# Closing a mixture-of-experts layer in groups of four tiles by batch entry, with eight gather buffers and normed values on ScalarE

## The chip, the cores and the metric

The kernel runs on one core of one Trainium2 chip, all in 32-bit floats. The metric is device time in microseconds (us) of one execution, the median of repeated runs. A core has a matrix engine (TensorE, PE in the profile; its weight loads are PEld), a vector engine (VectorE, DVE), a scalar engine (ScalarE, ACT), a fourth engine that here mostly issues indirect DMAs (GpSimd, POOL), and a queue that issues the other DMAs (SyncE, SP). Each engine works through its own queue of instructions in order. Where an instruction needs what another engine or a DMA makes, it waits on a semaphore, and all that is queued behind it waits too.

## The reference, cut to what matters

The input x is 4 batch entries of 1024 tokens of 128 values. Four layers follow each other, and each has two steps, `x = layernorm(x + f(x))`:

```python
x = ln(x + L0_attn(x)); x = ln(x + L0_ffn(x))   # cumulative-sum attention; linear in 6-bit steps
x = ln(x + L1_attn(x)); x = ln(x + L1_ffn(x))   # state-space scan; 16 experts, 4 per token, and a shared one
x = ln(x + L2_attn(x)); x = ln(x + L2_ffn(x))   # causal attention, 16 heads; 8 experts, 2 per token
x = ln(x + L3_attn(x)); x = ln(x + L3_ffn(x))   # Toeplitz gated unit; 32 experts, 4 per token, and a shared one
```

`ln` subtracts a token's mean and divides by the root of its variance plus 1e-5. The step of concern is the end of `L1_ffn`: for every token the outputs of its four experts, weighted, are added to x (which holds the shared expert's output already), and the sum is normed:

```python
x[t] += sum(wk[t, i] * y[pos[t, i]] for i in range(4)); x[t] = ln(x[t])
```

## The kernel before, in words

**Tiling.** The 4096 tokens are 32 tiles of 128 tokens (partitions) by 128 values. They are held by quarters of the sequence: quarter q has tokens 256q to 256q+255 of all four batch entries, which is eight tiles (QT), the first two of batch entry 0, the next two of entry 1, and so on. Part a is quarters 0 and 1 (16 tiles, the first half of the sequence), part r is quarters 2 and 3. Causal attention of layer 2 takes one half at a time, batch entry by batch entry: `l2_attn(0)` needs part a, `l2_attn(1)` needs both.

**Experts by lists.** A router (`l1_route`, L775) gives every token four places in a list that is sorted by expert. Tokens are scattered into the list in HBM by indirect DMA (`spread`, `indirect`, L1325), the experts run over it in tiles of 128 rows, and their results lie in HBM (`l1ya` for part a, `l1yr` for part r; `yg` is the tile that they are written from). `collect` (L1441) fetches them back. For each tile of tokens it takes one buffer "yt" of a pool `yp`, issues four gathers on POOL (indirect DMA, recorded at L1327) and later four multiply-adds on DVE (L1452). The pool's size is how many tiles can be under way: a gather into a buffer waits until the adds of the tile that had it before are done. `collect` issues the adds when a modelled landing time has passed, or when as many tiles are waiting as there are buffers, and a call of it adds all that it still has before it ends. `spaced(gen, 1, 2, 1.45)` (L1363) makes every gather wait for the landing of the one two before it; part r's gathers run so, part a's don't.

**Closing.** `l1_close` (L851) does this quarter by quarter: eight tiles collected, `norm` of the eight, one DMA that saves them in HBM (`xsave`, L858), and two times `turned` (L220), which is four PE transposes (L169) into a PSUM tile and one copy on ACT (L171) into xT, the transposed values that the next projections take.

**Norm.** `norm` (L189) takes a list of tiles. Per tile it has bn_stats and bn_aggr on DVE (L196, L197). `by="act"` takes the root on ACT (Sqrt, L200) and the reciprocal on DVE (L201); `by="dve"` takes Newton steps on DVE instead (L180 to L187, L204). Then the values: with `on_act=False`, one DVE instruction per tile (L213); with `on_act=True`, one small DVE instruction for all (`off`, L208) and one ACT instruction per tile (Identity with scale and bias, L211).

**What sets the order.** The program is recorded by generators that yield modelled costs. `mix(main, side, pace, drain)` (L242) records main and puts in as much of side as main's costs make due; `queued` (L232) keeps what is recorded from side behind what main has recorded so far on the same engine. A tile scheduler then orders each engine's instructions from these dependencies and a cost model. The stages around the change are written in `all` (L1957): at L1984 the shared expert and the experts of part a are the main work (`l1_experts`), beside which the chain of quarters 2 and 3 runs (`l2_norms`, `l0_ffn` L530, then `l1_attn` L648, both with `beside=True`). At L1985 `l1_close(a)` runs beside what is left of that chain and the making of layer 2's weights. Then comes `l2_attn(0)`, whose first PE work is transposes and projections of part a. At L1992 `l2_experts` (L1540) of layer 2's part a2 is the main work and `l1_close(r)` the side work; `l2_attn(1)` follows at L1999.

**Names in the steps.** In `l1_attn`, L669 forms the scan's inputs from a projection, L673 is the scan, L700 the residual add (two per quarter). In `l2_experts` a unit is one tile of the list: `gu` (PE, two products), `sg` (ACT, Silu, L1567), `hg` (DVE, L1569), four transposes into `tp`, `hT` (their copy, on ACT L171 or DVE L173 in turn), `yp` (PE); every four units `yg` is written (L1589) and a new list tile xg is transposed. `gu` and `sg` have two buffers, `hg` four, `hT` three. L979 adds an output bias to x inside `l2_attn`, L954 is its rotation, L933 to L935 are memsets of its value tile `va`, `sc` its scores. L1418 and L1419 read a count and branch over a rarely needed rest of the experts.

Of the kernel before, what the change touches and what calls it, by code (L numbers as in the profile page):

```python
# [30 lines left out]
QT = NT // NQT  # L31
# [9 lines left out]
E1, F1, NG1, TKG1, K1 = 16, 128, 4, 2, 4  # L41
# [33 lines left out]
class Kernel:  # L75
# [454 lines left out]
    def l0_ffn(self, qs, beside=False):  # L530

        nc, tc, x = self.nc, self.tc, self.x
        with ExitStack() as ctx:
            tp = self.pool(ctx, "l0ft", 4, right=True)
            qp = self.pool(ctx, "l0fq", 2, right=True)
            ps = self.side if beside else self.pool(ctx, "l0fps", 2, space=PSUM)
            tag = lambda t: "s" if beside else t
            for q in qs:
                t0 = q * QT
                xd = self.tile(qp, [P, QT, D], "xd")  # L540
                self.quantize(
                    tp,
                    xd.rearrange("p t d -> p (t d)"),
                    x[:, t0 : t0 + QT, :].rearrange("p t d -> p (t d)"),
                    QC // 32, beside,
                )
                yield (10.0,)

                lb = self.row["l0_b"].unsqueeze(1)
                if beside:  # L550
                    nc.gpsimd.tensor_tensor(
                        x[:, t0 : t0 + QT, :], x[:, t0 : t0 + QT, :], lb.to_broadcast([P, QT, D]), ALU.add
                    )
                for g in range(2):
                    xdT = self.tile(qp, [P, BLK], "xdT")
                    self.transposes(ps, xdT, [xd[:, g * 4 + k, :] for k in range(4)], tag=tag("tp"))
                    po = self.tile(ps, [P, 4, D], tag("po"))
                    if not beside:
                        self.mm(po, self.ident, lb.to_broadcast([P, 4, D]), True, False)
                    for k in range(4):  # L560
                        self.mm(po[:, k, :], xdT[:, k * P : (k + 1) * P], self.l0_wT, beside, beside or k == 3)
                    s = slice(t0 + g * 4, t0 + g * 4 + 4)
                    nc.vector.tensor_tensor(x[:, s, :], po, x[:, s, :], ALU.add)
                    yield (4.0,)
                self.norm(self.quarter(q), by="dve" if beside else "act", on_act=not beside)
                yield (6.0,)
                for g in range(2):
                    self.turned(ps, t0 + g * 4, tag=tag("tp"))
                yield (4.0,)
# [78 lines left out]
    def l1_attn(self, qs, beside=False):  # L648
        nc, tc, x, xT = self.nc, self.tc, self.x, self.xT
        tt, stt = nc.vector.tensor_tensor, nc.vector.scalar_tensor_tensor  # L650
        pw, wi, lh = self.l1_p, self.l1_w, self.l1_h
        rows = lambda a: a.rearrange("p (b t) -> p b t", b=B)
        steps = lambda a: a.unsqueeze(1).to_broadcast([P, B, TQ])
        with ExitStack() as ctx:
            tp = self.pool(ctx, "l1t", 2, right=True)
            ps = self.side if beside else self.pool(ctx, "l1ps", 2, space=PSUM)
            tag = lambda t: "s" if beside else "pu" if t == "pu" else "po"
            for q in qs:
                pu = []
                for h in range(2):  # L660
                    z = self.tile(ps, [P, BLK], tag("pu"))
                    self.mm(z, self.l1_b, xT[:, q * QC + h * BLK : q * QC + (h + 1) * BLK])
                    pu.append(z.rearrange("p (b t) -> p b t", b=B // 2))
                g = []
                for r in range(2):
                    b = self.tile(tp, [P, QC], "b")
                    for h in range(2):
                        hb = slice(h * B // 2, (h + 1) * B // 2)
                        tt(rows(b)[:, hb], pu[h], steps(wi[:, r, :])[:, hb], ALU.mult)  # L669
                    if q:  # L670
                        tt(rows(b)[:, :, 0], rows(b)[:, :, 0], lh[:, r, :], ALU.add)
                    s = self.tile(tp, [P, QC], f"g{r}")
                    nc.vector.tensor_tensor_scan(  # L673
                        s, self.l1_keep.rearrange("p b t -> p (b t)"), b, 0.0, ALU.mult, ALU.add
                    )
                    g.append(s)
                    yield (5.0,)
                if q + 1 < NQT:

                    ge = [rows(s)[:, :, TQ - 1] for s in g]  # L680
                    pr, pi = pw[:, 0, TQ - 1 :], pw[:, 1, TQ - 1 :]
                    u = self.tile(self.small, [P, 2, B], "lhu")
                    nc.vector.tensor_scalar(u[:, 0, :], ge[1], pi, self.l1_rho, ALU.mult, ALU.mult)
                    nc.vector.tensor_scalar(u[:, 1, :], ge[1], pr, self.l1_rho, ALU.mult, ALU.mult)
                    v = self.tile(self.small, [P, 2, B], "lhv")
                    nc.vector.tensor_scalar(v[:, 0, :], ge[0], pr, self.l1_rho, ALU.mult, ALU.mult)
                    nc.vector.tensor_scalar(v[:, 1, :], ge[0], pi, self.l1_rho, ALU.mult, ALU.mult)
                    tt(lh[:, 0, :], v[:, 0, :], u[:, 0, :], ALU.subtract)
                    tt(lh[:, 1, :], v[:, 1, :], u[:, 1, :], ALU.add)

                (tt if beside else nc.gpsimd.tensor_tensor)(rows(g[0]), rows(g[0]), steps(pw[:, 0, :]), ALU.mult)
                tt(rows(g[1]), rows(g[1]), steps(pw[:, 1, :]), ALU.mult)
                for h in range(2):
                    po = self.tile(ps, [P, 4, D], tag("po"))
                    for k in range(4):
                        c = slice((h * 4 + k) * P, (h * 4 + k + 1) * P)
                        for r in range(2):
                            self.mm(po[:, k, :], g[r][:, c], self.l1_c[:, r, :], r == 0, r == 1)
                    sl = slice(q * QT + h * 4, q * QT + h * 4 + 4)
                    tt(x[:, sl, :], po, x[:, sl, :], ALU.add)  # L700
                    yield (3.0,)
                self.norm(self.quarter(q), by="dve" if beside else "act", on_act=not beside)
                yield (6.0,)
                for h in range(2):
                    self.turned(ps, q * QT + h * 4, tag=tag("tp"))
                yield (4.0,)
# [144 lines left out]
    def l1_close(self, part, yp):  # L851

        nc, x = self.nc, self.x
        for q in range(part.q0, part.q0 + part.nq):
            yield from self.collect("l1", part, K1, yp, (q - part.q0) * QT, QT)
            self.norm(self.quarter(q))
            tl = slice(q * QT, (q + 1) * QT)
            nc.sync.dma_start(out=self.xsave[:, tl, :], in_=x[:, tl, :])  # L858
            yield (6.0,)
            for g in range(2):  # L860
                self.turned(self.side, q * QT + g * 4, tag="s")
                yield (1.5,)


# [1092 lines left out]
    def all(self):  # L1957
# [4 lines left out]
        with ExitStack() as ctx:  # L1962
            lgp = self.pool(ctx, "l2lg")
            self.l2_lg = self.tile(lgp, [P, NT, E2], "lg")
            with ExitStack() as early:

                self.l0_setup(early)
                self.l2_wr = self.load(lgp, self.ins["l2_wr"])
                with ExitStack() as room:
                    self.l0_room(room)  # L1970
                    self.run(self.l0_attn((0, 1)))
                    self.l1_setup()
                    self.zero_lists("l1")
                    self.run(self.l0_ffn((0, 1)))
                    self.run(self.l1_attn((0, 1)))

                    self.run(self.l1_route(a))
                    self.run(self.mix(self.l0_attn((2, 3)), self.spread("l1", a, K1)))
                self.zero_lists("l2", "l3")
                with ExitStack() as c2:  # L1980
                    wall = self.l1_wall(c2)
                    yp = self.pool(c2, "l1ya", 5, right=True)
                    side = self.chain(self.l2_norms(), self.l0_ffn((2, 3), True), self.l1_attn((2, 3), True))
                    self.run(self.mix(self.chain(self.l1_shared(a, self.l1_sw), self.l1_experts(a, wall)), side, 2.0, False))  # L1984
                    self.run(self.mix(self.abreast(self.l2_weights(), side), self.l1_close(a, yp)))  # L1985
# [237 lines left out]
```

## Time and profile before

| | |
|---|---|
| time, median of three runs | 1929.3 us (1927.78 to 1932.83) |
| the profiled execution's own time | 1937.33 us |
| its span in the profile | 1935.5 us |
| mean granted clock of TensorE | 0.896 |
| busy in the span | PE 1541.5, DVE 1199.2, ACT 900.6, POOL 690.3 us |
| gathers of part a (64) | start 459.3 to 557.3, median 947 ns each |
| adds of part a (64) | start 492.7 to 560.0, median 343 ns each |
| gathers of part r (64) | start 855.7 to 973.1, median 946 ns each |
| adds of part r (64) | start 892.5 to 980.4, median 346 ns each |
| first scores of `l2_attn(0)`, of `l2_attn(1)` | 574.44, 998.79 |

The times in the profile count from the start of the span of one execution. A row of a timeline has the start, the duration, the engine, the line of the kernel, the operation, what it writes and reads (names without buffer numbers), how many instructions run on end in the row, and in square brackets the idle time of that engine before it and what ended it. An engine that is idle before an instruction need not cost anything: it does so only where the work that sets the end passes through it. PE has the most busy time; where it is full, work of other engines beside it is hidden, and where it is not, the question is what it waits for.

### The profile page before, as it was taken

The page shows a single profiled execution, that of the slowest core. Times are in us where ns is not written, and L with a number is a line of the kernel's source. Part 1 is how long each engine was busy: PE and PEld are TensorE (multiplying, and loading weights), DVE is VectorE, ACT ScalarE, POOL GpSimd, SP SyncE. Part 2 cuts the span into 40 slices and gives each one's busy share as a digit, 9 for nine tenths or more (in the row PEclk, how much of TensorE's full clock was granted, in tenths as well). Part 3 has the DMA queues.
Part 4 walks back from the last instruction along what each step waited for, and adds up shares of the span by engine and source line. Part 5 has one row for each costly group of instructions (what it writes and reads, how often), then busy time and mean ns, then how long its engine had stood idle before and what let it go on. Part 6 is the DMA issues. An engine that isn't in the chain of part 4 may idle for free. (4 is left out here: it accounts for less than half of the span.)

```text
span 1935.5 us, 27095 instructions
## 1 busy us (share of the span) xinstructions
PE 1541.5 (80%) x9025; PEld 920.8 (48%) x9025; DVE 1199.2 (62%) x3491; ACT 900.6 (47%) x1349; POOL 690.3 (36%) x670
## 2 busy tenths in 40 slices
PE   7885677597847887989977878798798998999850
PEld 3332433385423345856632232333355757768650
DVE  8998698465766664635564565546442446866383
ACT  5876265243324554423336756564532236644330
POOL 2000148604630660265443000030536430567775
PEclk9897688798978998999988988898988999989985
DMA  9990002244430113632241000000452213425452
GB/s 297 288 288 10 1 17 86 87 126 133 159 129 18 60 63 129 183 96 73 78 137 32 1 1 1 2 23 1 159 213 83 66 28 93 141 68 167 122 147 61
DMA packets 215530, 187.10 MB, mean 97 GB/s; under 512 B 16528, under 2 KB 194064, under 8 KB 214864
## 3 DMA queue, kind: packets, MB, share of 16 engines
q1 hardware_dynamic: 194672, 142.29, 23.6%
q0 software_dynamic: 20704, 42.86, 7.3%
q8 instruction: 84, 1.38, 0.3%
q14 instruction: 70, 0.57, 0.1%
HBM read 88.49 MB, written 96.60 MB: 96 GB/s over the span
## 5 line engine op out<-in xcount | busy, mean ns | idle before, releaser
L1081 ACT ACTIVATE pr<-sc 128x1024 f32<-128x1024 f32 x288 | 279.4, 1021 | 175.2 <-PE sc L161 174.8
L161 PE MATMUL sc<-qm,kT 32*128 32x512 f32 (+3 forms) x1536 | 197.7, 559 | 16.7 <-ACT pr L1081 16.7
L161 PE MATMUL s<-pr,va 128*32 128x512 f32 (+3 forms) x1536 | 167.5, 532 | 19.0 <-DVE x L1019 10.2
L161 PE MATMUL gu<-ld,xgT 128*128 x640 | 165.1, 400 | 10.2 <-DVE hg L1812 5.9
L1087 DVE TENSOR_TENSOR pr<-pr,ld 128x512 f32<-128x512 f32 (+1 forms) x160 | 91.7, 581 | 105.6 <-ACT pr L1081 105.4
L161 PE MATMUL gu<-wall,xgT 128*128 x304 | 148.2, 612 | 2.0 <-ACT xgT L171 2.0
L161 PEld LDWEIGHTS sc<-qm,kT 32*128 32x128 f32 x1536 | 83.7, 194 | 112.4 <-issue 61.1
L161 PEld LDWEIGHTS gu<-ld,xgT 128*128 128x128 f32 x640 | 119.5, 198 | 34.7 <-DVE hg L1812 6.1
L1812 DVE TENSOR_TENSOR hg<-sg,gu 128x256 f32<-128x256 f32 x160 | 66.0, 417 | 92.0 <-ACT sg L1811 91.6
L173 DVE COPY hT<-tp 128x512 f32<-128x512 f32 x118 | 80.9, 686 | 66.2 <-PE tp L169 66.2
L1567 ACT ACTIVATE sg<-gu 128x512 f32<-128x512 f32 x76 | 45.4, 597 | 144.7 <-PE gu L161 143.6
L1811 ACT ACTIVATE sg<-gu 128x256 f32<-128x256 f32 x160 | 61.3, 385 | 107.7 <-PE gu L161 79.8
L171 ACT COPY xgT<-tp 128x512 f32<-128x512 f32 x99 | 58.0, 586 | 99.9 <-PE tp L169 99.8
L1327 POOL DMA_INDIRECT l1ra<-x,posl1a x64 | 79.8, 1246 | 61.3 <-DVE peq L1321 42.0
L1327 POOL DMA_INDIRECT l1rr<-x,posl1r x64 | 65.4, 1022 | 100.9 <-DVE posl1r L1302 70.8
L169 PEld LDWEIGHTS tp<-ld,hg 128*128 128x128 f32 x624 | 77.4, 141 | 49.0 <-issue 32.5
L1569 DVE TENSOR_TENSOR hg<-sg,gu 128x512 f32<-128x512 f32 x76 | 51.8, 682 | 78.9 <-ACT sg L1567 78.8
L1327 POOL DMA_INDIRECT l2rm<-x,posl2m x16 | 15.7, 983 | 236.8 <-DVE peq L1320 230.1
L169 PE MATMUL tp<-ld,hg 128*128 128x128 f32 x624 | 96.4, 275 | 3.7 <-DVE hg L1812 2.0
L1327 POOL DMA_INDIRECT l3ra<-x,posl3a x64 | 63.7, 996 | 93.3 <-DVE usedl3a L1315 51.0
L161 PEld LDWEIGHTS s<-pr,va 128*32 128x32 f32 x1536 | 37.1, 113 | 122.6 <-issue 78.4
L161 PE MATMUL yp<-ld,hT 128*128 x640 | 86.1, 276 | 2.3 <-DVE mv L197 1.5
(447 smaller groups left out, 3439.1 us busy)
## 6 DMA issues: line engine op xcount, KB each, us to landing
wall<-wall SPq DMA_DIRECT2D x16, 768.0 KB, 7.8
l3ra<-zero SPq DMA_DIRECT2D x1, 6144.0 KB, 25.5
ld<-in_l_w SPq DMA_DIRECT2D x2, 3072.0 KB, 10.6
wall<-we SPq DMA_DIRECT2D x24, 256.0 KB, 2.1
ld<-in_l_w SPq DMA_DIRECT2D x1, 6144.0 KB, 20.6
l1ra<-zero SPq DMA_DIRECT2D x1, 5120.0 KB, 19.6
l1rr<-zero SPq DMA_DIRECT2D x1, 5120.0 KB, 23.1
xg<-l3ra SPq DMA_DIRECT2D x20, 256.0 KB, 2.9
```

What stands on the lines that cost most here:

```text
L161: return self.nc.tensor.matmul(out, lhsT, rhs, start=start, stop=stop)
L169: nc.tensor.transpose(pt[:, k * P : (k + 1) * P], s, self.ident)
L171: nc.scalar.copy(dst, pt[:, : n * P])
L173: nc.vector.tensor_copy(dst, pt[:, : n * P])
L1081: nc.scalar.activation(pr, sc[h], AF.Exp)
L1087: nc.vector.tensor_tensor(d, d, cst["tril"].unsqueeze(1).unsqueeze(1).to_broadcast([P, 2, n, P]), ALU.mult)
L1327: ins = self.nc.gpsimd.indirect_dma_start(**kw)
L1567: nc.scalar.activation(sg, gu[:, 0, :], AF.Silu)
L1569: nc.vector.tensor_tensor(h, sg, gu[:, 1, :], ALU.mult)
L1811: nc.scalar.activation(sg, pg[:, :, 0, :], AF.Silu)
L1812: nc.vector.tensor_tensor(h[:, 2 * c : 2 * c + 2, :], sg, pg[:, :, 1, :], ALU.mult)
```

## The change

Three edits. The norms of quarters 2 and 3 in `l0_ffn` and `l1_attn` give their normed values on ScalarE (they keep the Newton steps on DVE). `l1_close` takes groups of four tiles: first the first four tiles (batch entries 0 and 1) of both quarters, then the last four (entries 2 and 3) of both; each group is collected, normed (values on ScalarE), saved and transposed on its own. The pool of gather buffers of part a has eight buffers instead of five; part r's keeps five.

```diff
@@ l0_ffn, and the same in l1_attn
-                self.norm(self.quarter(q), by="dve" if beside else "act", on_act=not beside)
+                self.norm(self.quarter(q), by="dve" if beside else "act", on_act=True)
@@ l1_close
-        for q in range(part.q0, part.q0 + part.nq):
-            yield from self.collect("l1", part, K1, yp, (q - part.q0) * QT, QT)
-            self.norm(self.quarter(q))
-            tl = slice(q * QT, (q + 1) * QT)
-            nc.sync.dma_start(out=self.xsave[:, tl, :], in_=x[:, tl, :])
-            yield (6.0,)
-            for g in range(2):
-                self.turned(self.side, q * QT + g * 4, tag="s")
+        for g in range(2):
+            for q in range(part.q0, part.q0 + part.nq):
+                t0 = q * QT + g * 4
+                yield from self.collect("l1", part, K1, yp, t0 - part.t0, 4)
+                self.norm([x[:, t0 + k, :] for k in range(4)], on_act=True)
+                nc.sync.dma_start(out=self.xsave[:, t0 : t0 + 4, :], in_=x[:, t0 : t0 + 4, :])
+                yield (3.0,)
+                self.turned(self.side, t0, tag="s")
                 yield (1.5,)
@@ all
-                    yp = self.pool(c2, "l1ya", 5, right=True)
+                    yp = self.pool(c2, "l1ya", 8, right=True)
```

In the order of the instructions after the change, POOL's gathers take the same places as before except that those of the last two tiles of part r stand behind the branch of L1419. On DVE the adds stand in other places, which the prediction names; t0 to t15 are a part's tiles in the order in which they are collected. SP has eight saves instead of four, and in `l2_experts` with the closing of part r ACT loads a table for Sqrt, or back from it, six times instead of two.

## Prediction

> **What bounds the kernel now.** I read the page's busy shares first, then busy time per 20-us window, then the timelines of PE, POOL and DVE in the two places where layer 1 is closed; the chain that ended last stays inside the last stage and says nothing here.
>
> ```profile
> PE 1541.5 (80%) x9025; PEld 920.8 (48%) x9025; DVE 1199.2 (62%) x3491; ACT 900.6 (47%) x1349; POOL 690.3 (36%) x670
> ```
>
> PE is the busiest engine, but a mean over stages doesn't price a closing. In the windows (window length, PE, PEld, DVE, ACT, POOL busy, then granted clock) the two closings differ:
>
> ```profile
> 520.00:540.00 20.00, 17.35 (x76) 11.03 (x76) 15.50 (x80) 5.75 (x11) 15.43 (x16) 0.91 0.78 281
> 540.00:560.00 20.00, 0.66 (x4) 0.42 (x4) 11.79 (x48) 1.50 (x3) 12.84 (x13) 0.57 0.36 107
> 560.00:580.00 20.00, 14.62 (x53) 6.64 (x54) 13.29 (x34) 5.86 (x8) 0.00 (x0) 0.75 0.17 68
> ...
> 930.00:950.00 20.00, 20.00 (x113) 13.92 (x111) 9.09 (x16) 6.94 (x13) 9.60 (x10) 1.00 0.31 82
> 950.00:970.00 20.00, 20.00 (x107) 13.46 (x106) 11.74 (x26) 5.60 (x10) 8.52 (x9) 1.00 0.15 41
> 970.00:990.00 20.00, 11.96 (x72) 9.09 (x71) 15.77 (x62) 6.26 (x9) 4.82 (x5) 0.83 0.40 118
> ```
>
> In the first half's closing (part a) PE stands still for 21 us while POOL gathers; in the second half's (part r) PE is full until about 980, so gathers, adds and norms lie beside l2_experts and only the tail after 980 is on the path. PE's timeline shows the hole (start, duration; in brackets the idle time and its releaser):
>
> ```profile
> 540.48 0.66 PE L169 MATMUL s<-ld,x 128*128 128x128 f32 x4 [0.68 <-ACT xT L171]
> 562.45 2.17 PE L169 MATMUL s<-ld,x 128*128 128x128 f32 x8 [21.31 <-DVE x L213]
> 564.41 4.94 PE L161 MATMUL s<-xT,w 128*128 128x512 f32 x8
> ```
>
> The named releaser is only the last link; behind it lie the last gather and its adds. POOL's stops in part a:
>
> ```profile
> 494.85 0.94 POOL L1327 DMA_INDIRECT yt<-l1ya,posl1a  x1 [9.52 <-DVE bn L196]
> ...
> 505.93 0.95 POOL L1327 DMA_INDIRECT yt<-l1ya,posl1a  x1 [1.30 <-DVE x L1452]
> ...
> 542.56 1.07 POOL L1327 DMA_INDIRECT yt<-l1ya,posl1a  x1 [2.05 <-DVE x L1452]
> ```
>
> From 459.3, 64 gathers at 1.25 us (their spacing where nothing stops them) would end at 539.4; the last starts at 557.30. So 9.5+1.3+2.1 us are waits for a buffer, about 5 us longer gathers, and the last add is at 560.05.
>
> **The change, part by part.**
>
> *Eight buffers in part a.* They remove the 9.5 and 1.3 us: t0 to t7 run 459.3 to 499.4, t8 to t11 until about 519.5. t12 then needs t4's buffer, hence t4's four adds. In the changed order of DVE these stand behind the residual adds (L700) of l1_attn's last quarter; before, 17 adds stood after that quarter's norms, at 540.34. So POOL's stop moves and may grow: what is late next is that quarter's chain.
>
> *Norms of the second half on ScalarE.* Eight L213 on DVE (2.14 us, at 501.65) become one L208 and eight L211. The trace has eight L211 in 3.19 us (at 100.38). Four such places: q2's and q3's in l0_ffn are hidden (after q3's at 463.06 PE waits for a weight load until 466.07). The one at 501.65 is not: DVE is free at about 503.4 and ACT does q2's L211 at 503.6 to 506.8, but then the first close group's table load (1.28), Sqrt (0.30) and four L211 (1.6) stand in ACT's queue ahead of the copies of q2's transposes, and that group's transposes in PE's queue. I get q3's first L669, behind them in PE's queue, at 518.2 instead of 508.65: +9.5. Given back: about 16 adds (4.3 us at 0.27, as 17 in 4.57 at 540.34) no longer lie inside that stretch, and up to 1 us of DVE's 4.19 of idle ahead of its first L700. The two L700 then come at about 530 and 533.6 (before 526.35 and 528.98). t4 is free at 535.9, t12's gathers run 536.1 to 541.1. t5 is free after the memsets and Newton steps (4.4 us, as at 533.85 to 538.29) and eight adds, at 542.7; t13 to t15 are 12 gathers, 15 us, last landing and add at 559.6 to 559.9. Before: 560.05. So POOL loses 13 us of stops and gains about the same at t12 and t13: −0.3.
>
> *Groups of four, batch order.* L1979's remaining adds are done earlier, −0.5 at the hole's end (four bn and adds in the tail instead of eight, against four L211 of 1.6 us for eight L213 of 2.2). Behind it stands one projection for one; the last group's transposes are ahead of the first scores in PE's queue, so that early batch entries lie ready changes nothing. +0.8 (0 to 2) for the longer norms inside l1_experts, where PE is at 14 to 18 of 20. Four saves more are 0.32 us each of SP's queue (the save at 987.55); behind one that waits for its norm stand, in part r, loads of l2_experts' rows, issued at 934.70 for the transposes of 946.70, so some 10 us early: 0, unless a norm is later than that. Part a: about **0, −4 to +4**.
>
> *Part r, five buffers.* The same order with the old pool. In the order in which tiles are now collected, gather t9 needs t4's adds, t10 t5's, t11 t6's, t12 t7's, t13 t12's, t14 t13's, t15 t8's. t4's adds stand behind the hg that ran at 927.89, so POOL stops until about 930.5 (its stops before: 9.15 us at 894.26, 8.38 at 955.17). From there 12 gathers lead to t12's first, four to its last; it lands 2.86 us later (855.68 to 858.54, where the gather two behind waits for it), its adds let t13 go, four gathers more, landing, add. With a spacing s that is 930.5 + 15s + 2.86 + 0.65 + 3s + 2.86 + 0.35 = 937.2 + 18s. s is 1.50 in the trace (the first 20 run 855.68 to 884.16; the later ones give the same without their stops), so t13 is added at 964.2. But the eight adds of t12 and t13 stand in DVE's queue *ahead* of t8's to t11's, between the hg of 943.57 and the hT of 955.65, so what is queued behind a waiting add is hg and hT of a PE that is full:
>
> ```profile
> 946.20 0.69 DVE L1569 TENSOR_TENSOR hg<-sg,gu 128x512 f32<-128x512 f32 x1 [1.96 <-ACT sg L1567]
> ...
> 952.79 0.69 DVE L1569 TENSOR_TENSOR hg<-sg,gu 128x512 f32<-128x512 f32 x1 [1.96 <-ACT sg L1567]
> ...
> 955.65 0.69 DVE L173 COPY hT<-tp 128x512 f32<-128x512 f32 x1 [0.74 <-PE tp L169]
> ```
>
> The rhythm is 3.05 us per unit. hg may be 3.35 us late (made 958.89 to 959.58, its gu buffer reused at 962.93) and hT 2.2 (955.65, wanted 958.50, 0.69 long). The hT of 949.55 goes behind t12's last add (956.2): 6.6 late, PE 4.4. That of 955.65 goes behind t13's (964.2): 8.5 late, PE **+6.4**, and a full PE doesn't make it up. At s = 1.28, the trace's shortest regular spacing, it is +2.4; at 1.65, the mean from 894.26 to 945.84 with its stops, +9.0.
>
> *Sqrt in part r.* Two norms of eight become four of four, and in l2_experts and its tail ScalarE loads a table six times instead of twice. The rows:
>
> ```profile
> 923.42 1.28 ACT L200 ACT_TABLE_LOAD   x1
> 925.06 0.30 ACT L200 ACTIVATE rstd<-mv,eps 128x8 f32<-128x8 f32 x1 [0.36 <-DVE mv L197]
> 925.90 1.28 ACT L1567 ACT_TABLE_LOAD   x1 [0.53 <-PE gu L161]
> ```
>
> Here the Trainium skill speaks against the change: the page "ScalarE: Activation LUTs" (What ACT_TABLE_LOAD costs) puts a switch at 1283 ns plus a drain of about 1380, 2.66 us in all, and its rules for kernel authors say to do all of one set before switching. By the page four more switches are 10.6 us of ACT, and each Silu behind one would come 2.7 late; by the row they are 5.1 us, with no drain to be seen beyond the 0.36 and 0.53 of idle, and the next Silu (927.19) is some 0.4 late while PE stays at 20.00 of 20. I take the row: ACT has 13 of 20 us free, 0 for two groups and +1 for the third, whose load, four L211 and transposes fall into the last units. By the page it would be +3.
>
> *Tail of r.* Four adds, norm and transposes instead of eight; ACT's L211 instead of L213; I have PE's first projection 9.1 us after the last yp, before 9.7 (979.90 to 989.59, 1.48 of it a weight load): −0.5. The last eight gathers move behind a branch on POOL; landed by about 981, before the experts end, some 6 us after 979.90: 0.
>
> **Sum.** Part a 0 (−0.3 −0.5 +0.8), part r +6.4 +1.0 −0.5: **+6.9**. On the profiled execution's own 1937.33 us (span 1935.5 and 1.83 around it) that is 1944.2. That execution lies 8.0 over the median of the three runs (1929.3); on the median the forecast is **1936.2**.
>
> **Rivals.** *Forecast as summed* (1932 to 1941): chance 0.50.
> *Not slower: the hole in part a closes earlier* (1929; 0.20). One mechanism: l1_attn's last quarter isn't held back by ACT, so t4's buffer is free when t11's gathers are through. Then POOL never stops there, the last gather ends up to 7 us sooner and PE's 21.3 becomes 14; −7 against part r's +6.9 is 0. The point is the start of part a's 49th gather: at 531 or before it wins all, at 536 nothing. For it: 13 us of stops are really there. Against it: table load and L211 ahead of q2's copies.
> *Slower still* (1943; 0.20). Part r's gathers at 1.65 (+9.5 for r) and part a's stop grows by 4: +13.5. For: that spacing is the trace's own beside a full PE; against: 4 us of it were waits for adds.
> *It does nothing* (1929 to 1932; 0.10): gathers at 1.28 when nothing else moves, +2.4 +0.5, and less if hg's slack is larger; the stop in part a only moved. [...]
>
> **How the numbers follow.** A measurement of this kernel tells 0.3% (5.8 us) from no change: 1923.5 to 1935.1. Faster needs the second and the fourth case together, 0.10; within are most of these two and a third of the first, 0.35; slower are the third and most of the first, 0.55. The range takes in half of the second case's spread below 1929 (1925) and reaches past the middle of the third (1944).
>
> **What would show it.** PE's idle before the transposes ahead of l2_attn(0): 21 right, 14 the rival. Part a's 49th gather at 536, after an L1452. q3's L669 at 518. In part r DVE waits for yt's landings between its hg, and PE loses some 6 us in 945 to 970; if it stays at 20.00 of 20, my part r is wrong. Six table loads in l2_experts, PE unmoved by the first four. The prediction fails above all if q2's chain slips by less than 9.5, or if part r's gathers run closer than 1.5.

## The result and the profile after

| | before | changed |
|---|---|---|
| median of 4 runs, us | 1931.07 (1927.78 to 1933.14) | 1950.78 (1950.57 to 1954.82) |
| profiled execution, own time / span | 1937.33 / 1935.5 | 1954.82 / 1952.8 |
| granted clock over the span | 0.896 | 0.891 |

The ratio is 1.0108 [1.0088, 1.0128]: the change costs about 20 us on this chip. The direction was forecast; the size was not (+5 to +7), and the time lies above the range. Later runs were on other chips, 16 to 18% slower, on which this cost is not seen in the whole time; the last section tells of it. Times of a kernel are therefore only set against `before` on the same chip, and lengths of stages are read within a trace. Every ratio with an interval is of the executions within 1.5% of the kernel's fastest, which on the slower chips, where they scatter by up to 3%, are 5 of 12 of the changed kernel and 21 of 23 of `before`, so that medians of all are given there too.

The page's busy line and the three windows around part r's closing, of the changed kernel (window; length; PE, PEld, DVE, ACT, POOL busy; granted clock, DMA share, GB/s):

```profile
PE 1544.0 (79%) x9025; PEld 924.8 (47%) x9025; DVE 1184.5 (61%) x3443; ACT 931.3 (48%) x1421; POOL 690.0 (35%) x670
```

```profile
930.00:950.00 20.00, 19.54 (x106) 13.03 (x104) 9.67 (x28) 11.06 (x19) 12.04 (x13) 1.00 0.28 80
950.00:970.00 20.00, 16.21 (x77) 11.22 (x78) 9.25 (x19) 3.93 (x7) 10.45 (x11) 0.83 0.25 63
970.00:990.00 20.00, 17.22 (x100) 12.22 (x99) 15.03 (x50) 10.03 (x16) 3.84 (x4) 0.98 0.19 56
```

The busy line hardly moved. In the windows, PE had 20.00 of 20 up to 970 before; now it loses some 4 us between 945 and 970, and what it does there runs at a lower clock. Milestones place the rest (us, from the timelines):

| | before | after | moved by |
|---|---|---|---|
| first scores of l2_attn(0), behind part a | 574.44 | 576.05 | +1.6 |
| first gate-and-up matmul of l2_experts | 863.89 | 863.65 | −0.2 |
| l2_experts to its last yp | 116.0 | 123.8 | +7.8 |
| last yp to the first scores of l2_attn(1) | 18.9 | 26.5 | +7.6 |
| first gather of l3yc, last stage | 1877.6 | 1892.6 | +15.0 |
| first to last gather of l3yc | 42.7 | 45.0 | +2.3 |

So part a's lateness is gone by 863; part r costs 15.4 us in two places of about equal size; and 2.3 come in a stage that the change doesn't touch.

**Inside l2_experts.** PE's timeline there (start, length, instruction; in brackets idle time and releaser):

```profile
948.94 0.60 PE L169 MATMUL tp<-ld,hg 128*128 128x128 f32 x4
953.79 2.08 PE L161 MATMUL yp<-wall,hT 128*128 x8 [4.25 <-DVE yg L1589]
955.66 3.35 PE L161 MATMUL gu<-wall,xgT 128*128 x4
...
959.29 1.06 PE L161 MATMUL yp<-wall,hT 128*128 x8
```

and DVE's:

```profile
951.56 0.35 DVE L1452 SCALAR_TENSOR_TENSOR x<-yt,wkl1r,x 128x128 f32<-128x128 f32 x1 [6.23 <-DMA yt<-l1yr,posl1r]
951.83 0.68 DVE L1569 TENSOR_TENSOR hg<-sg,gu 128x512 f32<-128x512 f32 x1
952.79 0.35 DVE L1452 SCALAR_TENSOR_TENSOR x<-yt,wkl1r,x 128x128 f32<-128x128 f32 x1 [0.28 <-DMA yt<-l1yr,posl1r]
953.05 0.68 DVE L1589 COPY yg<-yp 128x512 f32<-128x512 f32 x1
...
963.78 0.35 DVE L1452 SCALAR_TENSOR_TENSOR x<-yt,wkl1r,x 128x128 f32<-128x128 f32 x1 [1.64 <-DMA yt<-l1yr,posl1r]
```

DVE stands 6.2 us on the first add of t12, which its queue has ahead of the adds of t8 to t11; the gather for it began at 948.95 and landed only then. Behind t12's second add in the queue is the copy that empties yp (L1589), which has one PSUM buffer; PE cannot start the next yp until it has run. After 4.25 us without work PE is also slow: eight yp matmuls take 2.08 us instead of 1.06, four gate-and-up matmuls 3.35 instead of 1.88, together 2.5 us more, at a granted clock of 0.64 in 955 to 960. The third group's four transposes, which lay in the tail before, are in this stage now (1.05 us at 983.68 with 0.33 ahead). 4.25 + 2.5 + about 1 is the 7.8.

**In the tail.** PE again:

```profile
985.37 2.10 PE L161 MATMUL yp<-wall,hT 128*128 x16
995.85 0.86 PE L169 MATMUL s<-ld,x 128*128 128x128 f32 x2 [8.38 <-ACT x L211]
996.50 1.92 PE L161 MATMUL s<-xT,w 128*128 128x512 f32 x2
...
1006.66 4.39 PE L161 MATMUL s<-xT,w 128*128 128x512 f32 x6 [7.82 <-DVE rot L954]
```

The first projection is 9.03 us after the last yp (before 9.69), as forecast, although the transposes wait 8.4 us instead of 5.9: t14's and t15's adds start at 990.35, behind the branch of L1419 and va's memsets, with rows that landed long before. But two projections later PE stands still for 7.8 us, for want of a PSUM buffer that a rotation on DVE has to empty. DVE and SP's queue say why:

```profile
1005.21 0.74 DVE L1452 SCALAR_TENSOR_TENSOR x<-yt,wkl2a,x 128x128 f32<-128x128 f32 x2 [4.05 <-DMA yt<-l2ya,posl2a]
1005.86 0.75 DVE L954 SCALAR_TENSOR_TENSOR rot<-s,ld,ld 128x512 f32<-128x512 f32 x1
1006.52 0.75 DVE L979 TENSOR_TENSOR x<-x,rows 128x256 f32<-128x256 f32 x2
```

```profile
996.97 0.32 SPq L859 DMA_DIRECT2D xsave<-x  x1
```

Ahead of the first rotation stand four adds of layer 2's first results (wkl2a), whose gathers land at up to 1005.2. Before, that part of DVE's queue ran the four rotations first and those adds after, and the save was issued ahead of seven of the loads:

```profile
991.67 0.75 DVE L954 SCALAR_TENSOR_TENSOR rot<-s,ld,ld 128x512 f32<-128x512 f32 x1 [3.51 <-PE s L161]
998.22 0.34 DVE L1452 SCALAR_TENSOR_TENSOR x<-yt,wkl2a,x 128x128 f32<-128x128 f32 x1
```

```profile
987.55 0.32 SPq L858 DMA_DIRECT2D xsave<-x  x1
```

Now the last save stands behind eight loads of keys and values (3.2 MB by their sizes). L979, which here comes between the first rotation and the second, writes to x and must wait for that save. In this trace the adds hide its wait; an experiment below brings it out.

### The profile page after: what moved, and what is told of

Its sections match the earlier page's. It is cut to its first block, busy times and chain, and to the rows that moved or that the text cites. A ratio compares the mean times of both kernels' runs of the same rounds, so it can differ in the third digit from the quotient of the medians.

```text
span 1952.8 us, 27125 instructions
## 1 busy us (share of the span) xinstructions
PE 1544.0 (79%) x9025; PEld 924.8 (47%) x9025; DVE 1184.5 (61%) x3443; ACT 931.3 (48%) x1421; POOL 690.0 (35%) x670
## 5 line engine op out<-in xcount | busy, mean ns | idle before, releaser
L161 PE MATMUL s<-pr,va 128*32 128x512 f32 (+3 forms) x1536 | 163.1, 520 | 19.8 <-DVE x L1019 9.7
L211 ACT ACTIVATE x<-x,off,rstd 128x128 f32<-128x128 f32 x192 | 76.9, 481 | 36.3 <-DVE off L208 36.3
```

What stands on the lines that cost most here:

```text
L161: return self.nc.tensor.matmul(out, lhsT, rhs, start=start, stop=stop)
L211: nc.scalar.activation(x, x, AF.Identity, bias=off[:, t : t + 1], scale=rstd[:, t : t + 1])
```

## The experiments

Four sets; in each the stage lengths decide, since several edits act at once on the whole time.

**1. Which part carries it.** Five kernels with parts of the change; `before` was measured on the same chip (1930.5 to 1931.4). `r_old` is the change with the old closing, kept under another name, for part r:

```diff
-  self.mix(self.l2_experts(a2, wall2), self.spaced(self.l1_close(r, yp), 1, 2, 1.45))
+  self.mix(self.l2_experts(a2, wall2), self.spaced(self.l1_close_q(r, yp), 1, 2, 1.45))
```

`r_only` is `before` with the new closing for part r alone. `norms` is `before` with `on_act=True` in the second half's chain (twice), `bufs` is `before` with `"l1ya", 8`, and `a_close` is `r_old` with the chain's norms back at `on_act=not beside`.

> Part a closes as changed, with eight buffers and all norms on ScalarE; part r closes in the old way. The losing place is part r's closing: by that theory the time is that of before plus what part a costs, +1.6 us (0 to +4), about 1932, and the first scores of l2_attn(1) come at about 1000. Rival, part a's edits are the cause and what is seen in part r only follows from them: +12 to +20 stays. Rival, the range within which part a helps once part r doesn't lose: -3 or better.

> Part r closes in the changed way, all else is as before (part a by quarters with five buffers, norms of the second half on VectorE). Theory: the loss is part r's closing by itself: +14 to +17 on the kernel before, about 1946, and with the kernel that has only the rest of the change the two add up to the whole. Rival, the loss needs both (part r starts in another state after part a's new order): +8 or less here.

> Only the four norms of quarters 2 and 3 on ScalarE. Theory: most of what part a loses is here, since the row before showed 3.2 us on ScalarE for 2.1 on VectorE, with copies and products behind it: +2 us (0 to +4). Rival, VectorE is relieved of 8.6 us and gathers' adds come sooner: -2 to -4.

> Only the eight gather buffers of part a. Theory: POOL's stops before the tenth tile go, the stop behind the last quarter's chain stays: 0 to -3 us. Rival, more adds get in between VectorE's chain of the last quarter and delay it: +1 to +4.

> Part a closes in the changed way with eight buffers; norms of quarters 2 and 3 stay on VectorE and part r closes in the old way. Theory: without ScalarE's longer norms the closing of part a is about as before, 0 (-3 to +2), 2 us under the kernel that has the norms on ScalarE too. Rival, the closing of part a costs by itself: +5 to +7, as that kernel does.

| kernel | median, us | ratio to before | l2_experts | last yp to scores |
|---|---|---|---|---|
| r_old | 1937.36 | 1.0038 [1.0025, 1.0051] | 116.0 | 18.7 |
| r_only | 1948.64 | 1.0085 [1.0067, 1.0104] | 124.3 | 26.1 |
| norms | 1937.37 | 1.0032 [1.0020, 1.0044] | 116.0 | 18.8 |
| bufs | 1938.03 | 1.0035 [1.0020, 1.0050] | 116.0 | 18.3 |
| a_close | 1935.08 | 1.0020 [1.0009, 1.0032] | 116.1 | 18.7 |

Both losses in part r come with the new closing there and with nothing else: all four kernels without it have 116.0 to 116.1 and 18.3 to 18.8. Yet these four are 4 to 7 us above `before`, `bufs` too, in which only a pool grew. I had put these at 0 to +2, −3 at best; those were misses, and set 4 looks for their share. `r_only` (+17.2) and `r_old` (+6.9) were to add up to the whole; they make 24.1 for a measured 19.7, and the long gather of set 4, which both have, explains only 2.3 of that excess.

**2. What makes the stall in l2_experts.** Theories: the pool of five is too small; the tiles come too fast one after another; the table loads; the order of the batch entries; or the order in which DVE's queue has the adds. The edits:

```diff
# r_8
-  yp = self.pool(c2, "l1yr", 5, right=True)
+  yp = self.pool(c2, "l1yr", 8, right=True)
# margin_8: r_8, and in collect
-  late.append((t, yt, self.moved_by + 4.0))
+  late.append((t, yt, self.moved_by + (14.0 if part.name == "r" else 4.0)))
# slow_8: r_8, and part r's closing spaced at 1.9
-  self.spaced(self.l1_close(r, yp), 1, 2, 1.45)
+  self.spaced(self.l1_close(r, yp), 1, 2, 1.9)
# newton_r: no Sqrt in part r
-  self.norm([x[:, t0 + k, :] for k in range(4)], on_act=True)
+  self.norm([x[:, t0 + k, :] for k in range(4)], by="dve" if part.q0 else "act", on_act=True)
# loops: groups of four by quarters, the old order
-  for g in range(2):
-      for q in range(part.q0, part.q0 + part.nq):
+  for q in range(part.q0, part.q0 + part.nq):
+      for g in range(2):
# inorder: in part r, a tile's first add is kept behind the last add of the tile before it
+  if i == 0 and lay + part.name == "l1r":
+      for o in getattr(self, "added", []):
+          self.tc.add_manual_dep(got.ins, o, behind, reason="in order")
# ... (got is this add, behind an order-only tie, added the last add of the tile before)
```

`inorder_8` is `inorder` with eight buffers for part r, and `changed_again` is the changed kernel, for the same chip.

> The changed kernel with eight buffers for part r's gathers as well. Theory: the tiles whose adds stand early in DVE's queue are then fetched in time, so PE's 4.25 of idle in l2_experts and the slow products behind it are gone: 6 to 7 us less than the changed kernel, about 1944; the tail stays. Rival, the six table loads and the copies on ScalarE slow l2_experts: no change over 2 us; PE stays under 20 of 20 in the windows 950 to 970 and 930 to 950.

> The changed kernel with eight buffers in part r, its adds recorded 14 instead of 4 modelled us after the modelled landing. Theory: l2_experts is longer than before only because adds wait in DVE's queue for gathers that land later than modelled; with the margin DVE doesn't wait for yt within l2_experts, and from its first gu to its last yp it takes 117 us (before 116.0, changed 123.9), while the tail gets longer, as 20 adds come behind the branch. Rival, Sqrt loads, L211 and transposes on ScalarE and PE lengthen it: 121 or more.

> The changed kernel with Newton steps on VectorE in part r's norms, so that ScalarE loads no table in l2_experts. Theory: the tables cost next to nothing: l2_experts takes 122 to 124 us as in the changed kernel (123.9), PE's 4 us of idle before the yp at 953 stays. Rival[...]: 119 or less.

> The changed kernel with the two loops of the closing exchanged: both groups of four of a quarter first, then the next quarter, so not in the order of batch entries; groups of four, eight buffers and norms on ScalarE stay. Theory: batch order gives and takes nothing, since the last group's transposes stand ahead of the scores on PE in either order: the same as the changed kernel, ratio to before 1.009 to 1.0125, first scores 26 to 27 us after the last yp. Rival, batch order lets the first entries start early: 1.013 or more here.

> The changed kernel with eight buffers in part r, whose gathers are recorded as 1.9 us apart instead of 1.45 (they run at about 1.62 when nothing stops them). Theory: with a model slower than the chip no add is placed ahead of its landing, so DVE never waits for yt in l2_experts and from first gu to last yp it takes 116 to 118 us (changed 123.9; with eight buffers alone 127.0). The adds that then come behind the branch lengthen the tail. Rival, the copies and norms on ScalarE and the transposes on PE lengthen l2_experts: 120 or more.

> The changed kernel with one tie more: each tile's first add of part r is put behind the adds of the tile collected before it, so that VectorE's queue has them in the order of their gathers. In the changed kernel the adds of tiles 12 and 13 stand ahead of those of 8 to 11; in the kernels with more buffers, a longer margin or a slower model it is 12 and 13, 9 to 11, and 11 instead, and all of them still stalled. Theory: that inversion is the whole of l2_experts' loss: from first gu to last yp 116 to 117.5 us (before 116.0, changed 123.9), PE's 4.25 of idle gone, 6 to 7 us less than the changed kernel on the same chip; the tail stays at 26 us (26.5). Rival, gathers come late in any order because of five buffers: 121 or more.

> The same with eight buffers in part r. Theory: with the adds in order five buffers were enough, so no difference to the kernel with five: first gu to last yp 116 to 117.5. Rival, POOL's stops for a buffer were a cause of their own: clearly shorter than with five buffers.

> The changed kernel once more, beside the kernel with its adds in order, on the same chip. Theory: ratio to before 1.009 to 1.0125 as measured, with first gu to last yp 123 to 125 and 26 to 27 from there to the first scores. Rival, on a chip that is slower by 15 per cent the ratio moves towards 1, since other stages set more of the time there.

| kernel | l2_experts, us | of it first gu to first yp | PE's stops over 0.2 us after the first gu | part r's adds in DVE's queue, from t6 on |
|---|---|---|---|---|
| before | 116.0 | 8.4 | 0.68 | in order (neighbours such as 12 and 13 interleaved) |
| changed | 123.8 | 8.4 | 4.25 | 6 7 **12 13** 8 9 10 11 14 15 |
| r_8 | 127.0 | 8.4 | 6.22 | 6 **12** 6 **12** 7 **12 13** 8 ... |
| margin_8 | 122.3 | 8.4 | 3.65 | others: 0 1 **9** 2 ... |
| slow_8 | 127.9 | 12.6 | 6.67 | others: 3 **11** 4 5 ... |
| newton_r | 124.8 | 8.4 | 4.34 | as changed |
| loops | 127.3 | 10.1 | 5.04 | as changed |
| inorder | 117.0 | 8.4 | 0 | 0 to 15 in order |
| inorder_8 | 120.1 | 10.4 | 0.43 | in order |
| changed_again | 123.4 | 8.4 | 4.38 | as changed |

The time from first gu to first yp is the stage's entry, the same work in every kernel. Where it takes over 8.4 us PE starts the stage at a lower clock (0.79 over the first 10 us of `inorder_8`, 0.71 of `slow_8`, 1.00 of `inorder`). The adds begin later (at 28 us into the stage or after), so their order does not make that part.

`r_8` gave 1950.95, ratio 1.0103 [1.0081, 1.0125], nothing of what I expected of it: with more buffers the queue inverts elsewhere and PE stops in three places. `margin_8` and `slow_8` were to move adds away from their landings and made new inversions; both missed (one execution each, 2247.26 and 2276.8, beside `before` at 2247.77 and 2281.42 on their chips). `newton_r` has no table loads in the closing and keeps the stall, so those loads are not its cause (2241.0, one execution). `loops` keeps it too, so neither is the order of batch entries; its whole time (2277.87, 0.9957 [0.9913, 1.0001], where I expected 1.009 to 1.0125) says nothing of that, since on a chip like it the changed kernel has no such ratio either.

`inorder` takes nothing away and only forbids that a later tile's adds stand ahead of an earlier one's. The stall is gone, at five buffers. Its windows over that stage (columns as above; the stage's stretch in that trace):

```profile
1026.00:1046.00 20.00, 20.00 (x106) 13.27 (x105) 12.88 (x37) 10.24 (x19) 8.91 (x10) 1.00 0.27 77
1046.00:1066.00 20.00, 20.00 (x115) 14.16 (x114) 9.16 (x16) 6.68 (x12) 6.42 (x7) 1.00 0.22 62
```

PE is full at full clock again; 117.0 is `before` plus about 1 us for the four transposes. The stage is 6.4 us shorter than in `changed_again` on the same chip, as forecast (6 to 7). The whole times don't show this: the ratios to `before` are 0.9896 [0.9848, 0.9943] and 0.9902 [0.9846, 0.9958], the medians of all twelve 2224.86 and 2233.54 in ranges of 60 us. `inorder_8` (one execution, 2212.7) is 3.1 us longer than `inorder`: 2.0 are its slower entry, 0.4 idle time, the rest I can't place. Eight buffers bring nothing once the adds are in order. So an inverted queue is shown to be the cause. Why the scheduler inverts it is not: a collection of four never fills the pool of five, so the code's rule of adding a tile as soon as the pool is full no longer ties adds to gathers, but no run tried that by itself.

**3. What makes the tail.** Theory: DVE is late with the rotations because of layer 2's adds ahead of them. `hold` puts the whole chain that gathers and adds them off by 16 of the planner's us:

```diff
+  def put_off(self, gen, cost):
+      yield (cost,)
+      yield from gen
...
-  self.chain(self.spaced(self.rows_in(a2), 1, 2, 1.45), self.spaced(self.onward(a, True), 1, 2, 1.45)),
+  self.put_off(self.chain(self.spaced(self.rows_in(a2), 1, 2, 1.45), self.spaced(self.onward(a, True), 1, 2, 1.45)), 16.0),
```

`hold_8` has eight buffers besides. `nosave` leaves out part r's last save, `nosave_hold` does so and puts the chain off by 11:

```diff
+  if not (part.q0 and t0 == NT - 4):
       nc.sync.dma_start(out=self.xsave[:, t0 : t0 + 4, :], in_=x[:, t0 : t0 + 4, :])
```

> The changed kernel, with the fetching back of layer 2's first results recorded 16 modelled us later, so that in DVE's queue the eight first rotations stand ahead of its six first adds. Theory: 7 us (5 to 9) less than the changed kernel, 1943 to 1944, PE's 7.82 of idle between the first two projections gone, the first scores of l2_attn(1) at about 1006.5 instead of 1013.93; the 4.25 of idle in l2_experts stays. Rival, the tail is long because of ScalarE's norm and table load: within 2 us of the changed kernel, with first scores after 1012.

> Both at once: the changed kernel with eight buffers in part r and the first rotations ahead of layer 2's adds. If the two losses are separate and additive: 13 to 15 us less than the changed kernel, about 1936.5, and 4 to 7 over the kernel before, which is part a's 1.6 and the later start of part r's last adds (2.4). Rival, one hides behind the other (a shorter l2_experts only lengthens the wait for layer 2's gathers): 7 to 9 less, about 1943.

> The changed kernel without the last save of part r (which only a rarely run fallback reads), and with layer 2's first results fetched 11 modelled us later, so that the first rotations stand ahead of their adds. Theory: the rotation that PE waits for has two things in front of it that both end at 1005, the adds (waiting for gathers) and L979 (waiting for the last save, which lies behind 3.3 MB of loads). With both gone the first scores of l2_attn(1) come 14 us after the transposes of the last group begin, as before (985.79 to 998.79: 13.0); in the changed kernel it was 18.1, with the later fetching alone 16.6. Rival, the loads keep PE's own operand (w) back: 17 or more. The total is no measure here, since the chain behind the later fetching ends later.

> The changed kernel without the last save of part r, which only a rarely run fallback reads; the adds of layer 2's first results stay ahead of the rotations. Theory: two things block the rotation and both end at about the same time, so taking one away gives nothing: from the first transposes of the last group to the first scores 17 to 18 us (changed 18.1, without both 9.6). Rival, the save alone blocked: 13 or less.

| kernel | adds of layer 2 ahead | last save | transposes to first scores, us |
|---|---|---|---|
| before | no | early | 13.0 |
| changed | yes | late | 18.1 |
| hold | no | late | 16.6 |
| nosave | yes | none | 17.4 |
| nosave_hold | no | none | 9.6 |

`hold` was to win 7 us and lost 41 to the changed kernel (1992.12, 1.0311 [1.0286, 1.0336]); `hold_8` likewise (1994.4, 1.0321 [1.0290, 1.0351]; 16.2). The chain that it puts off feeds later stages: the first l3ra gather comes at 1384.0 instead of 1365.1, l3ya's at 1765.1 instead of 1725.5. As a whole time the run says nothing about the tail; as a trace it does. With the adds gone, DVE waits for something else, the same instruction that is L979 elsewhere:

```profile
1004.68 0.76 DVE L984 TENSOR_TENSOR x<-x,rows 128x256 f32<-128x256 f32 x2 [6.68 <-DMA xsave<-x]
```

It waits for the save, and behind it stands the second rotation. Each blocker removed alone brings 0.7 to 1.5 us, both removed 8.5: two waits that end together. PE in `nosave_hold` has hardly a hole left at the place of the 7.82:

```profile
1117.34 3.10 PE L161 MATMUL s<-xT,w 128*128 128x512 f32 x6 [0.42 <-DVE rot L960]
```

`nosave` and `nosave_hold` are one execution each, 2280.36 and 2259.08, beside 2281.42 and 2247.77 of `before` on their chips. With both gone the tail from last yp to scores is 17.9 us, 1.0 less than in `before`, although the transposes still wait 8.4 us for 5.9: the two blockers are the whole of the tail's loss. The chip does not make this: the instructions of `before` (`same`, set 4) on a slower chip have 12.9 from transposes to scores and a tail of 18.8.

**4. The time that no part explains.** In the last stage one gather on POOL takes longer, in three kernels here:

```profile
1877.59 3.44 POOL L1327 DMA_INDIRECT yt<-l3yc,posl3c  x1 [1.28 <-DVE x L1452]
```

```profile
1892.61 7.11 POOL L1327 DMA_INDIRECT yt<-l3yc,posl3c  x1 [1.53 <-DVE x L1452]
```

```profile
1876.72 7.11 POOL L1327 DMA_INDIRECT yt<-l3yc,posl3c  x1 [1.28 <-DVE x L1452]
```

They are `before`, changed and `bufs`, with the same instruction, wait and neighbours. The stretch of l3yc's gathers is 42.7 us in `before` and 45.0 in the others (44.9 in `norms`, 45.1 in `bufs`). `bufs` issues two instructions more, of some 27,000, and starts no later in that stage. Theory: it depends on the text of the program, so any edit brings it; rival: on the instructions that the edits bring. `same` is `before` with an unused method, `put_off`, added:

> The kernel before with an unused method added: the same instructions in the same order. What a comparison of two like kernels shows: ratio 1.000 within 0.0015. All kernels of these experiments show a long gather of 7.1 us in the last stage where the profiled run of before shows 3.4; if that is the run and not the kernel, it is 7.1 here too and the 2.3 us that separate the last stages are no effect of any edit. Rival: it is 3.4 here, and the edits cause it.

2236.33, ratio 1.000 [0.995, 1.0051], and 3.44 us for the gather. The rival stands: a kernel with the same instructions has the short gather, on another chip too. What in the instructions decides is open; no view names it. It makes 2.3 of the 4 to 7 us that `r_old`, `norms`, `bufs` and `a_close` are over `before`. The other 2 to 5 I can't place, and these traces can't show it: the profiled execution of `before` lay 6.3 over its own median, so the four profiled executions (1936.01 to 1938.76) are within 1.5 us of it. Whether a rebuilt `before` is as fast on the first chip was not measured; the interval of `same`, on another, is 11 us to either side.

## Why the prediction failed where it did

*Part a, "0, −4 to +4": right.* The 49th gather starts at 537.67, when t4's adds (L1452) have ended, between which the named bn runs (forecast 536); q3's L669 starts at 520.21 (forecast 518). POOL's stop moved instead of going, and the last transposes wait for their norm:

```profile
537.67 0.94 POOL L1327 DMA_INDIRECT yt<-l1ya,posl1a  x1 [9.63 <-DVE bn L196]
```

```profile
565.11 0.86 PE L169 MATMUL s<-ld,x 128*128 128x128 f32 x2 [8.86 <-ACT x L211]
```

The stop of 9.5 us is 9.6. PE's single hole of 21.3 is broken up by the earlier groups' transposes (17.4 us in five pieces, the last 8.86), but the first scores come 1.6 us later, and by the first matmul of l2_experts nothing is left of that. The rival that the hole closes earlier had its point at 531; it is out. One reading was off without effect: the longer gathers before are about 6.3 us, not 5, since 539.4 is where the 64th gather would end its spacing and 557.30 is where it starts.

*Part r's stall, "+6.4 +1.0": right to half a microsecond, by another victim and with luck.* 937.2 + 18s at 1.50 put t12's gathers at 948.5 to 953.0 and the end of t13's last add at 964.2; they are at 948.95 to 953.04 and 964.13. POOL went on 0.9 earlier than forecast (929.64) and its gathers were a little wider apart, 1.54 over that path. The sum was made for two hT that would be 6.6 and 8.5 late. What stopped PE was the copy out of yp, in DVE's queue behind the second add, and it stopped once. The working had neither the copy nor the slow restart of 2.5 us; a shorter idle time (4.25 for 6.4) and the restart nearly cancel, so that the size is luck. +7.8 stands against +7.4.

*Sqrt, by the row instead of the page "ScalarE: Activation LUTs": held.* Six loads stand in the stage, none in PE's idle time, and `newton_r` without them is not shorter (124.8 against 123.4 to 123.8), though its Newton steps put work on DVE instead. The +3 by the page is not there.

*The tail, "−0.5": wrong, and it is nearly all of the miss.* Measured +7.6. The step to the first projection was right (9.03 for a forecast of 9.1). The failed step is "Tail of r": it ends at PE's first projection and lets the rest follow as before, which the step for part a says in words ("Behind it stands one projection for one"). In part a that held; here PE stood still for 7.82 us two projections later. I had the order in which DVE's queue runs after the change, and did not read it past the closing, where layer 2's adds had moved ahead of the rotations. With it falls "Four saves more are 0.32 us each of SP's queue": I priced issue time and asked who waits behind a save in SP's queue, not who waits for the save itself, behind eight loads. Each of the two is enough to block: without the save 17.4 us from transposes to scores, without the adds 16.6, without both 9.6, for 18.1.

*The sum.* +15.4 in part r instead of +6.9, and +2.3 of the long gather in the last stage, which no step had, give the 17.5 between the profiled executions (1954.82 − 1937.33) to a few tenths. The medians differ by 19.7; `before`'s profiled execution lay 6.3 over its median, the changed one's 4.0.

*The rival "slower still" (1943)* had the sign and a wrong mechanism: the gathers were at 1.61 up to t12's first, but 1.54 over the path to t13's last add, and that place cost what the sum has. The range had no place for a late rotation and was too narrow for that.

## What to carry to other kernels

When a closing is cut into smaller pieces, read the new order of each in-order queue past the pieces, up to where the next stage runs freely, and ask of each instruction that can wait what stands behind it; a fixed order between adds cured here what three more buffers, wider spacing and later adds did not. A save has two prices, its place in the queue and the first writer that must wait for it; count the second from the loads queued ahead of it. Where two waits end together, taking away one shows next to nothing (0.7 to 1.5 us here, both 8.5): remove both before you drop either.

## What the hardware did that I had not expected

**PE's restart.** After 3.47 to 5.28 us of idle time PE runs at half speed (eight yp in 2.08 us instead of 1.06, in `hold_8`, `loops`, `changed_again`, the changed kernel, `newton_r` and `slow_8`; 1.68 in `r_only` after 4.74); the granted clock of the changed kernel is 0.52 from 953.79 to 958.80. After 2.54 us in `r_8` it does not, after 2.70 us in `margin_8` it does, soon after the restart (and after 3.07 us in `r_8`, 3.90 by the weight loads). The rows of `r_8`, then of `margin_8`:

```profile
936.54 0.97 PEld L161 LDWEIGHTS yp<-wall,hT 128*128 128x128 f32 x8 [2.78 <-DVE yg L1589]
936.55 1.16 PE L161 MATMUL yp<-wall,hT 128*128 x8 [2.54 <-DVE yg L1589]
```

```profile
995.27 0.42 PEld L169 LDWEIGHTS tp<-ld,hg 128*128 128x128 f32 x4 [3.52 <-DVE hT L173]
995.27 0.65 PE L169 MATMUL tp<-ld,hg 128*128 128x128 f32 x4 [2.70 <-DVE hT L173]
995.76 1.58 PE L161 MATMUL yp<-wall,hT 128*128 x8
```

The granted clock is 1.00 from 936.50 to 939.50 in `r_8` and 0.50 from 997.20 to 999.00 in `margin_8`. The two stops are nearly equal by PE's column, whose ends of matmuls are modelled, but not by the weight loads' (PEld): 2.78 and 3.52 us. The Trainium skill's page "TensorE: Matmul & The Clock Gate" (What's actually happening) puts the bound at about 3.4 us of idle time; with the idle time of PEld these rows lie on either side of it, with that of PE they do not. In the changed kernel the stall of 4.25 us cost about 6.75.

**Other chips.** On the first chip `before` takes 1931 us; on three others the same program has medians of 2247.77, 2281.42 and 2241.89, at granted clocks of 0.83 to 0.85. On the last of these the changed kernel has a ratio of 0.9902 [0.9846, 0.9958]; its median of all twelve executions is 2233.54 (2199.05 to 2260.21), 0.4% under that of `before` (2222.51 to 2265.42), and in such a scatter a win is not shown. That the loss of 1% is not seen there is all that can be said of the whole time. The two losses themselves are there: `same`, the instructions of `before` on one of these chips, has 117.7 for l2_experts (116.0 but for a slower entry of 10.1) and a tail of 18.8; the changed kernel on another has 123.4 and 26.2. What hides them in the whole time was not found, and whether `inorder` beats `before` on the first chip was not measured. The best that is shown is that it takes 6.4 us out of the changed kernel's stage.
